# Latent attention scores computed in row halves and row quarters of the systolic array, with a PSUM bank for each head

## The chip, the core and the metric

The kernel runs on one core of a Trainium2 chip. A core has a matrix engine (TensorE, "PE" in the profile, with its weight loads shown as "PEld"), three engines that work on vectors (VectorE "DVE", ScalarE "ACT", GpSimd "POOL") and SyncE ("SP"), which here issues most of the DMA transfers. Each engine runs its own instruction stream in order. TensorE writes its products to PSUM, which has eight banks of 512 fp32 values a partition; DVE and ACT read them from there. The metric is device time in microseconds, the median of several runs.

## The reference, cut to what matters

A decoder block with post-layernorm runs over 32 sequences of 256 tokens with 256 features, in fp32: latent self-attention, cross-attention to 120 context rows, and a mixture of experts with a shared expert. The change concerns the scores of the first part:

```python
Wdkv = x @ latent_w + latent_b                       # [32, 256, 72], keys and values
q = einsum('btc,hcl->bhtl', x, Wd_w) + Wd_b          # 16 heads of 72 features
scores = einsum('bhtl,bsl->bhts', q, Wdkv) / 4       # causal mask, softmax
y = einsum('bhts,bsl->bhtl', attn, Wdkv)
x = layernorm(x + y_as_rows @ out_w + out_b)
x = layernorm(x + cross_attention(x, ctx_1024))      # 16 heads of 64 features
x = layernorm(x + experts(x) + shared(x))
```

Keys and values are the same 72 latent features for every head. Since 72 is more than 64, the kernel stores a head's features as 64 (`LM`) and 8 (`LR`).

## The kernel before, in words

The sequences go through a software pipeline of rounds. Round n computes self-attention of sequence n, the end of it for sequence n-1, and cross-attention of sequences n-1 and n-2. `attention_round` (L795) writes out the order by hand, and within the blocks `manual_schedule` TensorE keeps exactly that order; SyncE keeps it in the start and round 0 only. The other engines' orders come from a scheduler that goes by priority; operations inside `urgent()` go ahead of others.

The sixteen heads are four groups (`g`) of four (`HG`). For a group, `queries` (L345) projects 4 x 64 query features in two blocks of 128 (two heads above each other). ACT (L366) and DVE (L373) move them from PSUM so that each head's 64 features lie in rows 0 to 63 of `qT`. The other 8 features of all 16 heads are projected once a sequence by `query_rest` (L333) into `q8`, and four DMAs a group (L352) copy each head's eight rows into rows 64 to 71 of `qT`. `keys` (L307) gives `kT` with 72 rows.

`scores` (L386) is called three times a group: bank 0 holds the first 128 queries of all four heads against 128 keys; banks 1 and 2 hold the other 128 queries of two heads each against 256 keys. Each matmul contracts 72 rows. DVE adds the mask (L402) and takes the negated maximum (L406); `softmax` (L409) runs an exponential per head on ACT (L412), the reciprocal on DVE (L419), and the scaling on POOL (L420). `turn` (L423) transposes the weights on TensorE, and `weigh` (L449) and `weigh_rest` (L472) multiply them with the values. The first uses two halves of the array's columns, the second four quarters of them. `latent_out` (L489) is the output projection.

For cross-attention, `cross_scores` (L558) already works in pairs: the even head in rows 0 to 63 of the array, the odd in rows 64 to 127, into two banks. `cross_turn`, `cross_weigh` (L596, two halves of the columns) and `cross_out` (L618) follow; `cross_keys` and `cross_values` prepare the context.

PSUM has two pools of banks: `"l"` with two, for `cross_scores`, and `"r"` with six, for everything else (L125). A step waits until a bank of its pool has been read.

After the last round the experts' work (`feed_forward`, L1011) is mixed into the remaining cross-attention by `fill`, and then runs alone.

Of the kernel before, what the change touches and what calls it, by code (L numbers as in the profile page):

```python
# [32 lines left out]
def decoder_kernel(  # L33
# [61 lines left out]
    mask = const.tile([P, 2 * P], F32, name="mask")  # L95
    nc.gpsimd.memset(mask, 0.0)
    nc.gpsimd.affine_select(
        out=mask[:, P:],
        in_=mask[:, P:],
        compare_op=ALU.is_ge,  # L100
        fill=NEG,
        base=0,
        pattern=[[-1, P]],
        channel_multiplier=1,
    )
# [94 lines left out]
    lat_sb = wp.tile([P, DC, L], F32, name="lat_sb")  # L200
    latb = wp.tile([L, 1], F32, name="latb")
# [13 lines left out]

    v_bufs = [wp.tile([P, TC, VW], F32, name=f"v_{k}") for k in range(2)]
# [4 lines left out]
    def first_weights():  # L221


        raw = ow_sb.rearrange("p a b -> p (a b)").rearrange("p (c n) -> p c n", c=DC)
        nc.sync.dma_start(out=lat_sb, in_=latent_w.rearrange("(c p) l -> p c l", p=P))
        nc.sync.dma_start(out=raw, in_=wd_w.rearrange("(c p) n -> p c n", p=P))
        nc.scalar.dma_start(out=latb, in_=latent_b.unsqueeze(1))
        nc.scalar.dma_start(
            out=wdbs[:, ZC - 1 : ZC], in_=wd_b[LM:, :].rearrange("l h -> (l h)").unsqueeze(1)
        )  # L230
        nc.scalar.dma_start(out=wdb_sb, in_=wd_b)
        nc.sync.dma_start(out=outb, in_=out_b.partition_broadcast(P))

    def order_weights():
# [10 lines left out]
        for d in range(DC):  # L245
            nc.vector.tensor_copy(
                wd_sb[:, d, H * LM :].rearrange("p (l h) -> p l h", h=H),
                by_head[:, d, :, LM:].rearrange("p h l -> p l h"),
            )
# [57 lines left out]
    def keys(s):  # L307

        st = states[s]
        pk = bank("r", [L, T], f"pk_{st['nm']}")  # L310
        project(pk, [(lat_sb[:, c, :], st["xT"][:, c, :]) for c in range(DC)])
        st["kT"] = sp.tile([L, T], F32, tag="kT", name=f"kT_{st['nm']}")
        with urgent():
            nc.scalar.activation(st["kT"], pk, AF.Identity, bias=latb)

    def values(s):
# [3 lines left out]
        for t in range(TC):  # L320
            nc.tensor.transpose(
                pv[:, t, :], st["kT"][:, t * P : (t + 1) * P], ident[:L, :L]
# [22 lines left out]
    def queries(s, g):  # L345

        st = states[s]
        qT = sp.tile([L, HG, T], F32, tag="qT", bufs=2, name=f"qT_{st['nm']}_{g}")
        st["qT", g] = qT
        for j in range(HG):  # L350
            h = g * HG + j
            nc.sync.dma_start(  # L352
                out=qT[LM:L, j, :], in_=st["q8"][h::H, :]
            )
# [8 lines left out]
        by_pair = qT[0:LM].rearrange("l (a two) t -> l a two t", two=2)  # L363
        with urgent():
            for a in range(2):
                nc.scalar.activation(  # L366
                    by_pair[:, a, 0, :],
                    pq[0:LM, a, :],
                    AF.Identity,
                    bias=wdbs[0:LM, c0 + a : c0 + a + 1],  # L370
                    scale=QSCALE,
                )
            nc.vector.scalar_tensor_tensor(  # L373
                by_pair[:, :, 1, :],
                pq[LM:P],
                QSCALE,
                wdbs[LM:P, c0 : c0 + 2].unsqueeze(2).to_broadcast([LM, 2, T]),
                ALU.mult,
                ALU.add,
            )  # L380
# [3 lines left out]
    BANKS = ((0, (0, 1, 2, 3)), (1, (0, 1)), (1, (2, 3)))  # L384

    def scores(s, g, k):  # L386
        st = states[s]
        t, js = BANKS[k]
        n, width = len(js), (t + 1) * P
        nm = f"{st['nm']}_{g}_{k}"  # L390
        pS = bank("r", [P, n, width], f"pS_{nm}")
        for a, j in enumerate(js):
            nc.tensor.matmul(  # L393
                pS[:, a, :],
                st["qT", g][:, j, t * P : (t + 1) * P],
                st["kT"][:, 0:width],
                start=True,
                stop=True,
            )
        sm = sp.tile([P, n, width], F32, tag="sm", bufs=5, name=f"sm_{nm}")  # L400
        m = mask[:, 2 * P - width :]
        nc.vector.tensor_tensor(  # L402
            sm, pS, m.unsqueeze(1).to_broadcast([P, n, width]), ALU.add
        )
        nmax = ap.tile([P, n], F32, tag="nmax", bufs=8, name=f"nmax_{nm}")
        nc.vector.tensor_reduce(nmax, sm, AX.X, ALU.max, negate=True)  # L406
        softmax(st, ("sm", g, k), sm, sm, nmax, n, width, nm)
# [15 lines left out]
    def turn(s, g, k):  # L423
# [9 lines left out]
        for j in range(HG):  # L433
            if k == 0:
                block = st["sm", g, 0][:, j, :]
            else:
                block = st["sm", g, 1 + j // 2][:, j % 2, (k - 1) * P : k * P]
# [86 lines left out]
    def cross_values(s, n):  # L524
        st = states[s]
        if n == 0:
            st["vx"] = ap.tile([S2, H, DH], F32, tag="vx", bufs=1, name=f"vx_{st['nm']}")
# [211 lines left out]


# [4 lines left out]
    def first_section(n):  # L745
        run(scores, n, 0, 0)
        run(scores, n, 0, 1)
        run(turn, n - 1, 3, 0)
        run(turn, n - 1, 3, 1)
        run(scores, n, 0, 2)  # L750
        run(turn, n - 1, 3, 2)
        run(queries, n, 1)
        run(cross_turn, n - 2, 4, 1, 0)
        run(cross_turn, n - 2, 4, 1, 1)
# [5 lines left out]
        run(cross_weigh, n - 2, 4)  # L760
        run(latent_out, n - 1)

    def last_section():

        weigh(B - 1, 2)
        for b in range(3):
            turn(B - 1, 3, b)
        weigh(B - 1, 3)
        weigh_rest(B - 1)
        latent_out(B - 1)  # L770
        for odd in range(2):
# [360 lines left out]
```

## Time and profile before

| | |
|---|---|
| median of 3 runs | 3464.92 us (3463.93 to 3467.61) |
| profiled execution, its own time | 3463.73 us |
| its span, first to last instruction | 3461.9 us |
| PE busy | 3435.6 us, 99% |
| weight loads busy | 2615.1 us, 76% |
| DVE, ACT, POOL busy | 1629.3, 1497.2, 1088.7 us |
| granted TensorE clock | 1.000 |
| one middle round | 75.0 us |
| the attention rounds end | at about 2390 us |

A row of a timeline has the start, the length, engine, line, operation, output<-inputs, shapes and how many instructions are merged (x). The shape `72*128 72x256` means 72 rows and 128 columns of the array and a moving operand of 256 columns. Ends of matmuls are modelled and overlap with the next ones, so the difference of two starts says more than the length. A row of a group has the busy time, the mean of one instruction in ns, and the idle time before it with what ended it. A row of the waits reads: engine, what waited, what it waited for, total us, times, longest us.

### The profile page before, as it was taken

To read this page: it belongs to the slowest core of one execution; us is meant where nothing else is said; L and a number is where in the kernel's file an instruction comes from. 1 tells how busy PE (TensorE), PEld (TensorE's weight loads), DVE (VectorE), ACT (ScalarE), POOL (GpSimd) and SP (SyncE) were. 2 spreads that over 40 slices of the span, in tenths; PEclk is the share of its full clock that TensorE was granted. 3 is DMA by queue.
4 is the path that set the end of the run, shared out by engine and by line. 5 is a ranking of instruction groups with operands and counts; after the bars stand their busy time and mean duration, and the time that the engine had idled before them with its cause. 6 is when DMAs were issued, how large, how long until landed. Compare 5 with 4: busy or idle time off the path is not lost.

```text
span 3461.9 us, 58143 instructions
## 1 busy us (share of the span) xinstructions
PE 3435.6 (99%) x21468; PEld 2615.1 (76%) x21468; DVE 1629.3 (47%) x3639; ACT 1497.2 (43%) x5456; POOL 1088.7 (31%) x1073
## 2 busy tenths in 40 slices
PE   8999999999999999999999999999999999999999
PEld 6888888888888888888888888887666656666655
DVE  4555555556555555654555565454311133221133
ACT  4556544555554555554455565445311111111111
POOL 2333322333332233332223333223344411444410
PEclk9999999999999999999999999999999999999999
DMA  3000000000000000000000000002455531455421
GB/s 97 17 16 17 17 17 25 18 20 17 17 17 20 24 17 20 17 17 16 20 24 20 17 17 17 16 17 86 100 123 124 131 97 62 117 123 123 105 82 52
DMA packets 144561, 164.42 MB, mean 47 GB/s; under 512 B 31384, under 2 KB 120216, under 8 KB 144280
## 3 DMA queue, kind: packets, MB, share of 16 engines
q1 hardware_dynamic: 119392, 126.09, 12.2%
q0 software_dynamic: 24576, 34.62, 5.7%
q8 instruction: 171, 2.80, 0.3%
q14 instruction: 110, 0.90, 0.1%
q10 hardware_dynamic: 312, 0.01, 0.0%
HBM read 105.61 MB, written 50.86 MB: 45 GB/s over the span
## 4 chain that ended last, share of the span: by engine, by line
PE 98%; ACT 0%; DMA 0%; DVE 0%; POOL 0%; SPq 0%; issue 0%; POOLq 0%; ACTq 0%
PE po L178 14%; PE pS L393 10%; PE pq L178 7%; PE pqx L178 7%; PE pd L178 6%; PE pg L178 6%; PE pu L178 6%; PE pz L458 5%; PE pT L438 5%; PE pL L565 4%; PE pc L604 3%; PE pxT L588 3%; PE pkx L178 3%; PE pu_s L178 3%; PE pg_s L178 3%; PE pvx L178 3%
## 5 line engine op out<-in xcount | busy, mean ns | idle before, releaser
L420 POOL TENSOR_TENSOR sm<-sm,rs 128x512 f32<-128x512 f32 x384 | 396.6, 1040 | 359.0 <-DVE rs L419 338.2
L412 ACT ACTIVATE sm<-sm,nmax 128x128 f32<-128x128 f32 (+1 forms) x1024 | 461.6, 466 | 18.6 <-DVE nmax L406 17.1
L420 POOL TENSOR_TENSOR xsm_x<-xsm_x,rs_x 128x480 f32<-128x480 f32 x256 | 252.4, 986 | 676.6 <-DVE rs_x L419 672.5
L412 ACT ACTIVATE xsm_x<-pL,nmax_x 128x120 f32<-128x120 f32 x1024 | 359.9, 375 | 124.3 <-DVE nmax_x L575 124.3
L393 PE MATMUL pS<-kT,qT 72*128 72x128 f32 (+1 forms) x2048 | 379.2, 328 | 3.7 <-DMA qT<-q 3.1
L152 POOL TENSOR_TENSOR rstd<-rstd,mhalf 128x2 f32<-128x2 f32 (+1 forms) x97 | 67.1, 692 | 934.1 <-DVE rstd L151 934.1
L393 PEld LDWEIGHTS pS<-kT,qT 72*128 72x128 f32 x2048 | 294.0, 191 | 21.7 <-ACT sm L412 2.8
L944 POOL DMA_INDIRECT acc<-eo,offs x128 | 200.8, 1569 | 342.3 <-DVE eo L941 313.4
L402 DVE TENSOR_TENSOR sm<-pS,mask 128x512 f32<-128x512 f32 x384 | 261.4, 681 | 70.7 <-PE pS L393 64.7
L178 PE MATMUL pq<-xT,wd_sb 128*128 128x256 f32 x1152 | 276.9, 381 | 0.0
L534 ACT COPY vx<-pvx 120x512 f32<-120x512 f32 x64 | 37.5, 585 | 549.5 <-PE pvx L178 549.5
L406 DVE TENSOR_REDUCE nmax<-sm 128x2 f32<-128x512 f32 (+1 forms) x384 | 258.6, 674 | 2.4
L178 PE MATMUL po<-ow_sb,zT 128*128 128x256 f32 x1152 | 257.2, 382 | 0.0
L1008 DVE TENSOR_TENSOR hT<-gl,pu 128x512 f32<-128x512 f32 x128 | 88.0, 688 | 341.6 <-PE pu L178 197.2
L178 PEld LDWEIGHTS po<-ow_sb,zT 128*128 128x128 f32 x1152 | 216.2, 190 | 40.1 <-DVE cxT L616 8.8
L178 PE MATMUL pg<-xeT,wg 128*128 128x512 f32 x512 | 240.8, 593 | 0.0
L178 PE MATMUL pu<-xeT,wu 128*128 128x512 f32 x512 | 240.6, 592 | 0.0
L178 PE MATMUL pqx<-x1T,wq_sb 128*128 128x256 f32 x1024 | 234.8, 382 | 0.0
L178 PEld LDWEIGHTS pq<-xT,wd_sb 128*128 128x128 f32 x1152 | 209.5, 191 | 25.0 <-issue 0.2
L178 PE MATMUL pd<-wd,hT 128*128 128x256 f32 x1024 | 226.6, 379 | 0.0
L178 PE MATMUL po<-wo_sb,cxT 128*128 128x256 f32 x1024 | 226.3, 379 | 0.0
L412 ACT ACTIVATION_READ_ACCUMULATOR xsm_x<-pL,nmax_x 128x1 f32 x1024 | 225.6, 220 | 0.0
(130 smaller groups left out, 5790.5 us busy)
## 6 DMA issues: line engine op xcount, KB each, us to landing
wg<-in_wg_dram SPq DMA_DIRECT2D x32, 512.0 KB
wu<-in_wu_dram SPq DMA_DIRECT2D x32, 512.0 KB
wd<-in_wd_dram SPq DMA_DIRECT2D x32, 512.0 KB
x<-in_x_dram SPq DMA_DIRECT2D x32, 256.0 KB
qT<-q SPq DMA_DIRECT2D x512, 8.0 KB
rows<-x SPq DMA_DIRECT2D x32, 256.0 KB
acc<-x SPq DMA_DIRECT2D x32, 256.0 KB
x2t<-x2T SPq DMA_DIRECT2D x32, 256.0 KB
```

The source lines that it names most:

```text
L178: nc.tensor.matmul(acc, lhsT, rhs, start=(i == 0), stop=(i == n - 1))
L393: nc.tensor.matmul(pS[:, a, :], st["qT", g][:, j, t * P : (t + 1) * P], st["kT"][:, 0:width], start=True, stop=True,)
L402: nc.vector.tensor_tensor(sm, pS, m.unsqueeze(1).to_broadcast([P, n, width]), ALU.add)
L406: nc.vector.tensor_reduce(nmax, sm, AX.X, ALU.max, negate=True)
L412: nc.scalar.activation(dst[:, a, :], src[:, a, :], AF.Exp, bias=nmax[:, a : a + 1], accum_out=rs[:, a, :],)
L420: nc.gpsimd.tensor_tensor(dst, dst, rs.to_broadcast([P, n, width]), ALU.mult)
L438: nc.tensor.transpose(pT[:, j, :], block, ident)
L458: nc.tensor.matmul(pz[odd * LM : (odd + 1) * LM, a, k * P :], st["v"][:, k, 0:LM], moving(st, g, 2 * a + odd, k), start=(k == 0), stop=(k ...
L565: nc.tensor.matmul(pLs[odd][:, j, :], st["qxT", c0][rows, j, t * P : (t + 1) * P], st["kxT"][rows, c0 + j, :], start=True, stop=True,)
L588: nc.tensor.transpose(pT[:, j, :], st["xsm", c0, t, odd][:, j, :], ident)
L604: nc.tensor.matmul(pc[odd * DH : (odd + 1) * DH, a, :], st["vx"][:, 2 * (c0 + j0 + a) + odd, :], st["xpt", c0, odd][:, j0 + a, :], start=True,
L944: nc.gpsimd.indirect_dma_start(out=acc[b], out_offset=self.rows(b), in_=eo[:, k, :], in_offset=None, compute_op=ALU.add,)
```

## The change

The scores of a head are now two sums into one bank. The eight extra features of four heads are contracted in the four row quarters of the array at once: head j of a group uses rows 32j to 32j+31. For that the columns of the extra query weights, and so the rows of `q8`, are put in the order (j, l, g), and a new tile `kr` holds the eight key rows in the same places, with zeros in the rows of the other groups. `keys` projects them four times (`LW` = 96 columns), and `place_keys` spreads them with four DMAs. The 64 main features are contracted in the two row halves: the even head in rows 0 to 63, the odd in rows 64 to 127. The queries can then stay as they were projected, and a copy of the keys, `kD`, is kept in the lower half. The DMAs from `q8` to `qT` fall away.

`scores` is called once a group and takes four `"r"` banks, one for each head, 128 + 256 columns. The mask has three blocks. The maximum, the reciprocal and the scaling run over all four heads, once for 128 columns and once for 256. The round is laid out anew: `cross_scores` follows each `scores`, a `cross_weigh` or `weigh` precedes three of the four, and `cross_out` is in the second quarter of the round. The start of the kernel has a written order on all engines.

```diff
+    LW = LM + HG * LR
+    lat_sb = wp.tile([P, DC, LW], F32, name="lat_sb")
...
+    kr = wp.tile([P, NG, T], F32, name="kr")
+    nc.gpsimd.memset(kr, 0.0)
...
+        nc.scalar.dma_start(out=latb[0:L], in_=latent_b.unsqueeze(1))
+        for j in range(1, HG):
+            nc.scalar.dma_start(
+                out=latb[LM + j * LR : LM + (j + 1) * LR], in_=latent_b[LM:].unsqueeze(1)
+            )
+        by_column = wd_b[LM:, :].rearrange("l (g j o) -> j (l g) o", j=HG, o=1)
+        for j in range(HG):
+            nc.sync.dma_start(
+                out=wdbs[j * 32 : (j + 1) * 32, ZC - 1 : ZC], in_=by_column[j]
+            )
+        nc.vector.tensor_copy(
+            lat_sb[:, :, L:].rearrange("p c (j l) -> p c j l", l=LR),
+            lat_sb[:, :, LM:L].unsqueeze(2).to_broadcast([P, DC, HG - 1, LR]),
+        )
...
     def keys(s):
-        pk = bank("r", [L, T], f"pk_{st['nm']}")
+        pk = bank("r", [LW, T], f"pk_{st['nm']}")
+        st["kD"] = sp.tile([P, T], F32, tag="kD", name=f"kD_{st['nm']}")
         with urgent():
             nc.scalar.activation(st["kT"], pk, AF.Identity, bias=latb)
+            nc.vector.tensor_scalar(st["kD"][LM:], pk[0:LM], latb[0:LM], None, ALU.add)
+    def place_keys(s):
+        for g in range(NG):
+            nc.sync.dma_start(out=kr[g::NG, g, :], in_=states[s]["kT"][LM:, :])
...
     def queries(s, g):
-        for j in range(HG):
-            h = g * HG + j
-            nc.sync.dma_start(
-                out=qT[LM:L, j, :], in_=st["q8"][h::H, :]
-            )
...
-            nc.vector.scalar_tensor_tensor(
-                by_pair[:, :, 1, :],
...
+    SEG = (slice(0, P), slice(P, 3 * P))
+    def scores(s, g):
+        pS = [bank("r", [P, 3 * P], f"pS_{nm}_{j}") for j in range(HG)]
+        for t in range(TC):
+            for j in range(HG):
+                rows = slice(j * 32, (j + 1) * 32)
+                nc.tensor.matmul(
+                    pS[j][:, SEG[t]],
+                    st["q8"][rows, t * P : (t + 1) * P],
+                    kr[rows, g, 0 : (t + 1) * P],
+                    start=(t == 0),
+                    stop=False,
+                )
+        for a in range(2):
+            for t in range(TC):
+                for odd in range(2):
+                    rows = slice(odd * LM, (odd + 1) * LM)
+                    k = st["kD"] if odd else st["kT"]
+                    nc.tensor.matmul(
+                        pS[2 * a + odd][:, SEG[t]],
+                        st["qT", g][rows, a, t * P : (t + 1) * P],
+                        k[rows, 0 : (t + 1) * P],
+                        start=False,
+                        stop=(t == TC - 1),
+                    )
+        sm = sp.tile([P, HG, 3 * P], F32, tag="sm", bufs=2, name=f"sm_{nm}")
+        for j in range(HG):
+            nc.vector.tensor_tensor(sm[:, j, :], pS[j], mask, ALU.add)
+        for t in range(TC):
+            nc.vector.tensor_reduce(nmax[:, t, :], sm[:, :, SEG[t]], AX.X, ALU.max, negate=True)
+            for j in range(HG):
+                nc.scalar.activation(
+                    sm[:, j, SEG[t]], sm[:, j, SEG[t]], AF.Exp,
+                    bias=nmax[:, t, j : j + 1], accum_out=rs[:, t, j, :],
+                )
+            nc.vector.reciprocal(rs[:, t], rs[:, t])
+            block = sm[:, :, SEG[t]]
+            nc.gpsimd.tensor_tensor(
+                block, block, rs[:, t].to_broadcast([P, HG, (t + 1) * P]), ALU.mult
+            )
...
-            st["vx"] = ap.tile([S2, H, DH], F32, tag="vx", bufs=1, name=f"vx_{st['nm']}")
+            st["vx"] = ap.tile([S2, H, DH], F32, tag="vx", bufs=2, name=f"vx_{st['nm']}")
...
+    def attention_round(n):
+        run(cross_weigh, n - 2, 0)
+        scores(n, 0)
+        run(cross_scores, n - 2, 4, 1)
+        (turn n-1,3 x3; cross_turn n-2,4,0 x2; weigh n-1,2; weigh n-1,3; weigh_rest n-1)
+        if routed(n):
+            route((n - 3) // BQ)
+        run(latent_out, n - 1)
+        (load and load_context n+1; cross_turn n-2,4,1 x2; cross_values n-1 x2)
+        (cross_keys n,0; turn_x1 n-1; queries n,1; score; cross_queries n-1 x4)
+        run(cross_weigh, n - 2, 4)
+        scores(n, 1)
+        run(cross_scores, n - 1, 0, 0)
+        (turn n,0 x3; queries n,2; cross_out n-2)
+        scores(n, 2)
+        run(cross_scores, n - 1, 0, 1)
+        (turn n,1 x3; cross_turn n-1,0,0 x2; queries n,3; turn_x2 n-2)
+        (turn_x, keys, query_rest n+1; weigh n,0; weigh n,1)
+        scores(n, 3)
+        run(cross_scores, n - 1, 4, 0)
+        (turn n,2 x3; place_keys, values n+1; queries n+1,0)
+        (cross_turn n-1,0,1 x2; cross_keys n,1)
...
+    every = {getattr(mybir.EngineType, n) for n in ("PE", "SP", "DVE", "Activation", "Pool")}
+    with tc.manual_schedule(engines=every):
         load(0)
...
-        unit.hT = fp.tile([P, FC, cols], F32, tag="hT", name=f"hT_{unit.nm}")
+        unit.hT = fp.tile([P, FC, cols], F32, tag="hT", bufs=1, name=f"hT_{unit.nm}")
```

In the diff, lines in brackets of `attention_round` name the calls in short. The last section and the mixing of the first experts with the end of cross-attention are reordered to match.

## The prediction

> **What bounds the kernel now.** I read the page's first and fourth parts first, then TensorE's waits.
>
> ```profile
> span 3461.9 us, 58143 instructions
> PE 3435.6 (99%) x21468; PEld 2615.1 (76%) x21468; DVE 1629.3 (47%) x3639; ACT 1497.2 (43%) x5456; POOL 1088.7 (31%) x1073
> PE 98%; ACT 0%; DMA 0%; DVE 0%; POOL 0%; SPq 0%; issue 0%; POOLq 0%; ACTq 0%
> ...
> PE pk L178 <- DVE xT L172: 6.9, 1, 6.9
> PE pxT L168 <- DMA x<-in_x_dram: 4.0, 1, 4.0
> PE pS L393 <- DMA qT<-q: 3.1, 2, 2.4
> ```
>
> TensorE is the bound and waits for almost nothing: the chain is 98% PE, its waits sum to some 18 us, nearly all in the first 30. So what counts is the time from one matmul's start to the next. The page's means (379 ns for pS) are modelled latencies and overlap, so I take differences of starts. Here is TensorE's timeline around one group of four heads; each fp32 matmul leaves two records, called passes here, each with its weight load.
>
> ```profile
> 1514.89 1.92 PE L393 MATMUL pS<-kT,qT 72*128 72x128 f32 x12
> 1516.65 1.04 PE L438 MATMUL pT<-ident,sm 128*128 128x128 f32 x8
> 1517.53 1.03 PE L393 MATMUL pS<-kT,qT 72*128 72x256 f32 x4
> 1518.39 0.60 PE L438 MATMUL pT<-ident,sm 128*128 128x128 f32 x4
> ```
>
> The scores take 1516.65-1514.89 plus 1518.39-1517.53 = 2.62 us. In the records' starts a pass of 128 columns takes 0.112 us and one of 256 takes 0.216: 8 x 0.112 + 8 x 0.216 = 2.62. The eight transposes between (one record each) take 0.88, 0.109 each. Two existing steps show what packing does: the cross scores (two halves of 64 rows) and weigh_rest (four columns' quarters).
>
> ```profile
> 1511.24 0.81 PE L178 MATMUL pqx<-x1T,wq_sb 128*128 128x256 f32 x3
> 1511.98 1.16 PE L565 MATMUL pL<-kxT,qxT 64*128 64x120 f32 x16
> 1513.06 0.48 PE L178 MATMUL pqx<-x1T,wq_sb 128*128 128x256 f32 x1
> ...
> 1558.43 2.81 PE L479 MATMUL pzr<-pt,v 128*32 128x256 f32 x64
> 1561.17 0.44 PE L604 MATMUL pc<-xpt,vx 120*64 120x256 f32 x2
> ```
>
> The 16 pL records are 8 pairs, both halves starting 7 ns apart and the next pair 0.111 later: 0.89 us, and 1513.06-1511.98 = 1.08 shows 0.19 more. That is the price of changing the array's division. The 64 pzr records are 16 quads: 8 x 0.216 + 8 x 0.109 = 2.60 of the 2.74 shown. A quad costs what one pass costs.
>
> **The stream of the scores.** scores (L386) loses 8 passes of each width. It gains 4 heads x 2 blocks of 8 features in quarters, so with quads at one pass's price 2 x 0.112 + 2 x 0.216 = 0.656 us; and 64 features in halves, four pairs of two passes: 4 x 0.112 + 4 x 0.216 = 1.312. Together 1.968 against 2.624: -0.656 a group, x 128 groups = **-84.0 us**. Pairs of 64 rows are seen in pL, at 120 columns. Four row quarters into four banks at once are not seen here; the nearest row is pzr, four column quarters. The bounds are 0.656 (quads) and 1.312 (only pairs run together: +84.0 in all, no saving).
>
> **A rule against it.** The Trainium skill, "TensorE: Matmul & The Clock Gate", section Measured speedup vs the span model, gives four row tiles of 32 rows a measured 3.07 times, not 4. By it the quarters take 2.624/3.07 = 0.855 us, +0.199 a group, +25.5 us in all, and the forecast would be 3442. I take the row: pzr's quads lose nothing in an unbroken stream. The rule stays as a case.
>
> **Changes of division.** From the starts of all records, as the drain ahead plus the weight load laid bare: full to 64 columns 0.145, 64 to 32 columns 0.124, 32 to 64 columns 0.164, columns to full 0.20, full to row halves 0.189, 64 columns to row halves 0.196, row halves to the turns 0.155, to a projection 0.202. A round now has 13: weigh, weigh_rest, cross_weigh, latent_out (0.637), four visits of cross_scores (0.391, 0.344, 0.344 and, with weigh ahead and keys behind, 0.543): 2.26 us. After the change there are 18. Scores enter quarters (0.196, once 0.189), then halves (0.196), cross_scores follows in halves for nothing, and the turns leave (0.155): 0.547, 0.547, 0.540, 0.547. Columns are entered for weigh 2 (0.145), weigh_rest (0.124), left for latent_out (0.20), and entered for cross_weigh twice and weigh 0 (3 x 0.145): 3.09 us. +0.826 a round, x 32 = **+26.4 us**. Quarters are put at what halves cost, as the exposed load has the same 128 columns; 0.1 either way is 13 us.
>
> **The softmax behind the scores.** All four heads now go through in one block each of 128 and 256 columns. DVE: four adds of 384 (between 0.41 at 256 and 0.69 at 512, 0.47 net of overlap), reduces of 0.6 and 1.2. POOL: 1.04 and, by 733 ns at 256 and 1040 at 512, 1.65. ACT's exponentials are the same. All lie beside PE; what matters is that they are in time. The stretches between scores in the middle round, one row each, the last one long:
>
> ```profile
> 1514.90:1524.90 10.00, 10.00 (x82) 9.09 (x81) 8.21 (x18) 8.26 (x38) 5.09 (x5) 1.00 0.02 5
> 1524.90:1539.30 14.40, 14.40 (x122) 11.82 (x121) 10.14 (x20) 10.54 (x42) 6.39 (x7) 1.00 0.06 20
> 1539.30:1549.00 9.70, 9.70 (x79) 8.78 (x78) 7.70 (x18) 9.22 (x40) 5.09 (x5) 1.00 0.03 8
> 1549.00:1589.90 40.90, 40.90 (x287) 32.73 (x287) 15.27 (x36) 13.25 (x48) 6.44 (x8) 1.00 0.08 24
> ```
>
> The columns are length, PE, PEld, DVE, ACT and POOL busy, clock and DMA. ACT is at 9.22 of 9.70 in the third, so a tight place exists. Moving cross_out (6.9 us) into the first stretch makes the distances from the end of scores to the next cross_scores 13.3, 12.7 and 11.1 us, by the same prices. The third is: cross pairs 0.89, turns 1.46, values 0.14, queries 1.73, cross_turn 0.87, cross_keys 1.78, cross_weigh 1.87, scores 2.36. Before that next cross_scores both "l" banks must have been read by ACT. ACT starts about 2.0 us after scores end (last two adds, first reduce), then needs, by distances of starts, 4 x 0.39 + 4 x 0.51 for exponentials, 8 x 0.35 for the cross ones, one late turn copy 0.47, queries 0.73, cross turn 0.46, kxT 0.44: 8.5. That ends at 10.5 against 11.1. The turns need 2.0 + 1.56 + 2.04 + 1.7 of copies + 0.2 + 1.65 = 9.2 of 12.4. So the cover is 0.6 us, and an order of ACT that runs late by more goes straight to PE. Queued behind a waiting cross_scores are turn, cross_turn and weigh; next late would be latent_out. I take 0.2 us for 30 rounds, **+6 us**, between 0 and 1.5 a round (0 to 45).
>
> A second rule, "TensorEngine Tiling (Array Packing)", section PSUM Bottleneck, says that evacuation may become the bottleneck after packing. DVE reads pS for 4 x 0.47 = 1.9 us a group, against 3 x 0.6 = 1.8 now, in stretches of at least 11 us of which it is busy about 8; by the row it adds nothing, by the rule the 2 us before the softmax could grow, which the 0 to 1.5 holds.
>
> **Four banks at once.** Six "r" banks rotate. Ahead of the four scores come two cross_weigh or weigh tiles (or a query and cross_out), 1.7 us or more of PE after the next older ones (pqx, pq8, pkx, turns). Their copies take 0.6 to 0.7. Cost 0; if a copy queues behind exponentials, up to 0.5 a round, in the range above.
>
> **Keys.** keys projects 96 columns for 72, same passes; kD is one DVE operation of some 0.41 and takes the place of four of 0.69 (L373). place_keys issues 4 DMAs of 32 KB a round on SP, where queries issued 16 of 8 KB. kr has one buffer: the fourth waits for the last quarters of scores(n, 3), and loads and stores queued later on SP wait with it. Due at scores(n+1, 0), 10 us on. In the first round the rows from q (ready 15.92) let pS start at 17.91: some 2 us a small transfer, 2 to 4 here, hidden. Were it late, PE would wait at once. One hT buffer costs nothing: the next write follows pu, which PE runs after the last down. A second vx only frees.
>
> **Start and first rounds.** The waits for qT in round 0 go (3.1 DMA, 0.4 DVE and some unattributed: -4). But round 0 has no cross work between scores: turn(0, 0) comes 5.7 us after scores(0, 0) end, its second block is ready after 7.5; the same at turn(0, 1): about +3.5. In round 1 cross_scores(0, 0, 1) comes 6.2 us after its forerunner, whose banks are read after some 10: +4. First weights: four small SP DMAs, three on ACT, one DVE copy; DVE now in written order, so xT's copy no longer waits behind the weights (the 6.9 above), but query_rest still needs them at about 10 us. 0. Sum **+3.5**, between -4 and +10. The tail has the same work in another order: 0, 3 us either way.
>
> **Sum.** -84.0 + 26.4 + 6 + 3.5 = -48.1 against the profiled execution's 3463.7 (span 3461.9 and 1.8 around it): 3415.6. The median is 1.2 above it: **3417**.
>
> **Rivals.** (1) Quads by the rule: 3442. For it: no row of four row tiles here; against it: pzr. (2) ACT and the "l" banks late by 1 us a round: +24 on my sum, 3441; for it: ACT's 95% in one stretch and the 0.6 us of cover; against it: the longer first stretch, and PE's waits for ACT today are nearly none. The two overlap in time. (3) Slower: the quarters do not stream, the four tiles' writes to four banks go two by two. Place: the eight passes ahead of each group. Price: 3417 + 84 = 3501. It decides from 48/84 of the way, a quad at 1.57 passes. For it: no evidence that four banks are written at once; against it: pairs into two banks lose nothing. A milder form of (2), 1.8 us a round, ends at the old time. (4) No change: gain and late softmax cancel, 3465.
>
> **How the numbers follow.** My forecast with its own range (3400 to 3436, stalls 0 to 0.8 a round) 0.58; (1) or (2) 0.19; within 0.2% 0.07; slower 0.16, by (3) 0.09 or (2) worse than 1.8. 0.2% (7 us) is about what a measurement of this kernel can tell. Faster 0.77, same 0.07, slower 0.16. The range starts at 3398: no stall and first rounds at -4 give 3403, and 0.03 less a change of division 5 less again. It reaches to 3490, short of most of (3), so that about 2 in 10 is left out.
>
> **What would show it.** Records of pS in 32-row form, four starts within some 20 ns and the next quad 0.112 or 0.216 later: the stream; 0.15 or more, the rule. First-pass starts at the entry: 0.2. Waits of PE pL on ACT xsm_x, or of pT on POOL sm, over 6 us in all: rival 2. Waits of pS on DMA kr: place_keys late. A sum over PE of starts that is right with a total that is not would put the error in the start or tail.

## The result and the profile after

The changed kernel takes 3585.61 us (median of 4 runs, 3583.82 to 3585.84) against 3466.18 for the kernel before on the same chips: ratio 1.0344, 95% interval 1.0326 to 1.0362. It is 119 us slower where 48 us faster was forecast. The profiled execution took 3585.64 us. From the page of the changed kernel, its span, TensorE's busy time and the chain that ended last:

```profile
span 3583.9 us, 60589 instructions
...
PE 3471.2 (97%) x23516; PEld 2572.2 (72%) x23516; DVE 1538.5 (43%) x3416; ACT 1481.1 (41%) x5456; POOL 1064.9 (30%) x947
...
PE 75%; DVE 14%; ACT 8%; issue 1%; POOL 1%; DMA 0%; SPq 0%; POOLq 0%; ACTq 0%; DVEq 0%
```

The chain was 98% PE; now almost a quarter of it runs through DVE and ACT. PE's busy share fell only from 99% to 97%: the modelled ends of matmuls cover a part of each wait. TensorE's waits in the changed kernel, with their total, their number and the longest:

```profile
PE pk L180 <- DVE xT L174: 56.1, 32, 1.9
PE pz L497 <- DVE pt L481: 5.7, 25, 0.2
PE pT L477 <- POOL sm L446: 5.6, 3, 2.2
PE pxT L170 <- DVE pt L481: 5.5, 29, 0.2
PE px2T L170 <- ACT pt L483: 5.1, 30, 0.2
PE pL L604 <- ACT xsm_x L454: 4.8, 5, 1.4
```

What happened once before (6.9 us, in the start) happens in every round: `keys` waits for the copy of `xT`, which `turn_x` has only just handed to DVE. The lines of `pxT` and `px2T` are the same lateness, seen from PSUM banks that ACT and DVE have not read yet. The middle round, cut at the starts of its four `scores` (columns: length, PE, PEld, DVE, ACT and POOL busy, granted clock, DMA):

```profile
1502.40:1515.70 13.30, 13.30 (x102) 11.49 (x100) 6.15 (x13) 8.61 (x37) 4.18 (x4) 1.00 0.01 1
1515.70:1533.00 17.30, 15.09 (x129) 11.33 (x128) 10.83 (x25) 9.80 (x40) 7.58 (x8) 0.90 0.16 53
1533.00:1544.80 11.80, 11.80 (x116) 9.64 (x114) 8.52 (x23) 7.24 (x29) 2.21 (x2) 1.00 0.02 4
1544.80:1581.40 36.60, 36.60 (x293) 29.01 (x292) 13.94 (x32) 15.10 (x57) 8.24 (x8) 1.00 0.04 11
```

The forecast had 13.3, 12.7 and 11.1 us for the first three. The first is exact, the second is 4.6 us too long, and in it alone the granted clock is below 1. Here is that stretch in the timeline of the changed kernel:

```profile
1515.74 0.94 PE L410 MATMUL pS<-kr,q 32*128 32x128 f32 x16
1515.85 0.69 DVE L667 TENSOR_TENSOR r<-po,x 128x512 f32<-128x512 f32 x1 [0.65 <-PE po L180]
...
1516.61 0.37 PE L422 MATMUL pS<-kT,qT 64*128 64x128 f32 x1
...
1518.03 1.05 PE L604 MATMUL pL<-kxT,qxT 64*128 64x120 f32 x16
1518.56 0.73 DVE L156 TENSOR_SCALAR x<-r,mv,rstd 128x256 f32<-128x256 f32 x2 [0.81 <-POOL rstd L154]
...
1519.21 1.94 DVE L431 TENSOR_TENSOR sm<-pS,mask 128x384 f32<-128x384 f32 x4
...
1521.96 0.40 ACT L437 ACTIVATE sm<-sm,smax 128x128 f32<-128x128 f32 x1 [6.97 <-DVE smax L435]
...
1525.90 0.68 DVE L174 COPY xT<-pxT 128x512 f32<-128x512 f32 x1
...
1526.72 0.64 PE L180 MATMUL pk<-xT,lat_sb 128*96 128x256 f32 x2 [1.85 <-DVE xT L174]
```

The layernorm of `cross_out` (L667 to L156) now stands directly ahead of `scores(n, 2)`, so DVE is still busy with it, and for 0.81 us waiting for POOL's step of it, when the scores are done. The four adds of the mask begin at 1519.21, 1.2 us after PE has gone on to the cross scores. ACT, idle for 6.97 us, gets its first exponential 3.9 us after the scores end (1518.03 to 1521.96); in the stretch before this one it is 2.3. Everything that the two engines do behind it (copies of the turns, `x2T`, `xT`) is late by that, and `turn_x` has nothing between itself and `keys` any more. Here they start 2.5 us apart, 1.85 of it the wait. In the profile of before they start 6.1 us apart, with two `weigh`, a `cross_weigh` and a `cross_scores` between them:

```profile
1531.43 0.60 PE L168 MATMUL pxT<-ident,x 128*128 128x128 f32 x4
1531.96 2.82 PE L458 MATMUL pz<-pt,v 128*64 128x256 f32 x32
1534.61 1.90 PE L604 MATMUL pc<-xpt,vx 120*64 120x256 f32 x16
1536.44 1.16 PE L565 MATMUL pL<-kxT,qxT 64*128 64x120 f32 x16
1537.53 1.08 PE L178 MATMUL pk<-xT,lat_sb 128*72 128x256 f32 x4
```

The clock, by the same columns, in three neighbouring windows of that stretch:

```profile
1524.00:1527.40 3.40, 1.35 (x8) 0.99 (x8) 2.58 (x6) 3.40 (x13) 2.39 (x3) 1.00 0.05 17
1527.40:1530.80 3.40, 3.40 (x14) 2.07 (x14) 0.83 (x3) 3.40 (x19) 2.78 (x3) 0.51 0.21 68
1530.80:1534.20 3.40, 3.40 (x50) 2.44 (x48) 0.87 (x2) 0.97 (x4) 1.06 (x2) 0.99 0.11 29
```

PE was busy for 1.35 of 3.40 us, and in the next 3.4 us its clock is half. `pk`, `pq` and the first `pz` in it take 1.7 us longer than the same passes elsewhere. So the stalls of 2.9 us in this stretch cost 4.6, which is what it is too long by.

**Where the time went.** For every pass I subtract from the distance to the next start what such a pass takes in an unbroken stream (0.109 to 0.112 us at 128 columns, 0.216 at 256, 0.429 at 512). The excess goes to a half-speed window (3.4 us in which the granted clock is 0.5) if it lies in one, else to a change of division if the neighbour has another one, else to waits.

| us | changes of division | waits | half-speed windows | span |
|---|---|---|---|---|
| before | 75.0 | 20.7 | 0 | 3461.9 |
| after | 116.8 | 149.0 | 36.1 | 3583.9 |
| e3_both | 126.2 | 80.7 | 10.2 | 3499.1 |
| e5_old_scores | 92.5 | 107.8 | 15.9 | 3582.4 |
| e10_cover_weigh | 117.0 | 60.8 | 5.5 | 3465.6 |
| e13_both_on_vector | 116.8 | 33.1 | 5.1 | 3437.0 |

After less before: 41.8 + 128.3 + 36.1 - 84.0 (the stream, as forecast) = +122.2; the spans differ by 122.0. The saving was made, and 206 us were lost elsewhere. A wait that ends beside a change of division is booked as a change, so the line between these two columns is rough.

### The profile page after: what moved, and what is told of

It reads as the page before. It is cut to its first block, busy times and chain, and to the rows that moved or that the text cites. A ratio compares the mean times of both kernels' runs of the same rounds, so it can differ in the third digit from the quotient of the medians.

```text
span 3583.9 us, 60589 instructions
## 1 busy us (share of the span) xinstructions
PE 3471.2 (97%) x23516; PEld 2572.2 (72%) x23516; DVE 1538.5 (43%) x3416; ACT 1481.1 (41%) x5456; POOL 1064.9 (30%) x947
## 4 chain that ended last, share of the span: by engine, by line
PE 75%; DVE 14%; ACT 8%; issue 1%; POOL 1%; DMA 0%; SPq 0%; POOLq 0%; ACTq 0%; DVEq 0%
PE po L180 13%; PE pqx L180 6%; PE pd L180 6%; PE pu L180 6%; PE pg L180 6%; DVE sm L431 5%; PE pq L180 5%; PE pz L497 4%; DVE smax L435 3%; ACT sm L437 3%; PE pu_s L180 3%; PE pg_s L180 3%; PE pfo L180 3%; PE pvx L180 3%; PE pzr L518 2%; ACT xsm_x L454 2%
## 5 line engine op out<-in xcount | busy, mean ns | idle before, releaser
L446 POOL TENSOR_TENSOR sm<-sm,srs 128x512 f32<-128x512 f32 (+1 forms) x256 | 375.4, 1466 | 1448.4 <-DVE srs L444 1255.2
L437 ACT ACTIVATE sm<-sm,smax 128x128 f32<-128x128 f32 (+1 forms) x1024 | 459.2, 451 | 586.7 <-DVE smax L435 586.7
L180 PE MATMUL pq<-xT,wd_sb 128*128 128x256 f32 x1152 | 294.5, 399 | 1.8 <-DVE wd_sb L266 1.8
L431 DVE TENSOR_TENSOR sm<-pS,mask 128x384 f32<-128x384 f32 x512 | 249.5, 547 | 90.5 <-PE pS L422 90.2
L180 PEld LDWEIGHTS pq<-xT,wd_sb 128*128 128x128 f32 x1152 | 221.5, 201 | 32.4 <-DVE wd_sb L266 2.6
L435 DVE TENSOR_REDUCE smax<-sm 128x4 f32<-128x512 f32 (+1 forms) x256 | 232.2, 947 | 4.4
L180 PE MATMUL pqx<-x1T,wq_sb 128*128 128x256 f32 x1024 | 227.0, 380 | 0.0
L180 PEld LDWEIGHTS po<-wo_sb,cxT 128*128 128x128 f32 x1024 | 194.5, 190 | 26.9 <-issue 0.5
L180 PEld LDWEIGHTS pqx<-x1T,wq_sb 128*128 128x128 f32 x1024 | 194.4, 191 | 26.9 <-issue 0.8
L180 PEld LDWEIGHTS pd<-wd,hT 128*128 128x128 f32 x1024 | 192.1, 190 | 27.5 <-DVE hT L1034 1.8
```

What stands on the lines that cost most here:

```text
L180: nc.tensor.matmul(acc, lhsT, rhs, start=(i == 0), stop=(i == n - 1))
L431: nc.vector.tensor_tensor(sm[:, j, :], pS[j], mask, ALU.add)
L435: nc.vector.tensor_reduce(nmax[:, t, :], sm[:, :, SEG[t]], AX.X, ALU.max, negate=True)
L437: nc.scalar.activation(sm[:, j, SEG[t]], sm[:, j, SEG[t]], AF.Exp, bias=nmax[:, t, j : j + 1], accum_out=rs[:, t, j, :],)
L446: nc.gpsimd.tensor_tensor(block, block, rs[:, t].to_broadcast([P, HG, (t + 1) * P]), ALU.mult)
```

## The experiments

Each ratio is against the kernel before on the same chip. The line numbers are those of the changed kernel unless an edit shifts them.

### Two orders in the second stretch

**e1_turnx_early** moves `turn_x` away from `keys`, ahead of `cross_out`; **e2_norm_early** moves `cross_out` into the stretch's beginning, so that its layernorm is over before `scores(n, 2)`; **e3_both** does both.

```diff
         run(cross_scores, n - 1, 0, 0)
+        run(cross_out, n - 2)             # e2, e3
         for b in range(3):
             turn(n, 0, b)
         queries(n, 2)
+        run(turn_x, n + 1)                # e1, e3
-        run(cross_out, n - 2)             # e2, e3
...
         run(turn_x2, n - 2)
-        run(turn_x, n + 1)                # e1, e3
         run(keys, n + 1)
```

> The changed kernel with turn_x(n+1) moved ahead of cross_out(n-2), so that keys(n+1) no longer follows it at once. Theory 1 (adjacency: keys right behind turn_x makes TensorE wait 1.9 us a round for the copy of xT, and that wait brings the windows at half clock): the wait of pk on xT goes (61 us), the windows at half clock of the rounds go (some 32 us), 3585 falls to about 3490. Theory 2 (DVE late: the layernorm behind cross_out holds DVE while the adds of scores(n, 2) wait, and everything after is late): the wait moves on to the next steps of the same stretch (turn_x2, query_rest, weigh), and the time stays above 3545.

> The changed kernel with cross_out(n-2) moved ahead of turn(n, 0) and queries(n, 2), 3.4 us earlier, so that its layernorm is over when scores(n, 2) end; turn_x and keys stay together. Theory 2 (DVE late): the adds of scores(n, 2) start about 2.4 us earlier against the scores, the wait of pk on xT falls to 0.6 us or less and the waits of px2T and weigh go: about 3480. Theory 1 (adjacency): the wait of pk stays at 0.9 us or more, as the copy takes 0.7 after the transposes, and only the half clock goes: about 3520.

> Both moves. If the two causes are all there is, the stream of the prediction is left: 3417 to 3440, under the time of before. If the softmax in one block for four heads is late in itself, waits of turn, cross_scores or weigh remain and it stays above 3460.

e1: 3527.97 us, ratio 1.0180 (1.0163 to 1.0197). e2: 3512.29, 1.0136 (1.0119 to 1.0153). e3: 3498.45, 1.0091 (1.0074 to 1.0107). Both causes are real: 58 and 73 us. They overlap, since together they give 87. The two largest steady waits of PE in e1:

```profile
PE pc L643 <- ACT xpt L631: 10.8, 30, 0.4
PE pz L497 <- DVE pt L481: 5.8, 25, 0.2
```

In e1 the wait of `pk` for `xT` is gone, and the excess in half-speed windows falls from 36.1 to 5.2 us. But another wait, of `cross_weigh` for a copy on ACT, has grown and now leads the list: that step takes 2.91 us a round, in the changed kernel 2.51, elsewhere 1.88. In e2 `pk` still waits for `xT` (33.7 us, 32 times, at most 1.1) and the half-speed windows cost 8.5: the stall is as frequent and shorter. The softmax of that stretch is in time again: the adds begin while the scores still run, and ACT starts 2.3 us after they end (1476.57).

```profile
1476.11 1.95 DVE L431 TENSOR_TENSOR sm<-pS,mask 128x384 f32<-128x384 f32 x4 [0.24 <-PE pS L422]
1476.57 1.05 PE L604 MATMUL pL<-kxT,qxT 64*128 64x120 f32 x16
1478.87 0.40 ACT L437 ACTIVATE sm<-sm,smax 128x128 f32<-128x128 f32 x1 [3.64 <-DVE smax L435]
```

e3 has neither, and still takes 76.1 us a round where the kernel before takes 75.3 (rounds 3 to 30). So I had found the first two causes, not all.

### Which half of the change brings the waits

**e4_old_round** puts the new `scores` into the order of the old round and tail; **e5_old_scores** puts the old scores (with the old keys, queries and softmax, six `sm` buffers instead of five) into the new round and tail.

```diff
 # e4, in the old round
-        run(scores, n, 0, 0)
-        run(scores, n, 0, 1)
-        run(turn, n - 1, 3, 0)
-        run(turn, n - 1, 3, 1)
-        run(scores, n, 0, 2)
-        run(turn, n - 1, 3, 2)
+        run(scores, n, 0)
+        for b in range(3):
+            run(turn, n - 1, 3, b)
 # e5, in the new round
-        scores(n, 0)
+        for k in range(3):
+            scores(n, 0, k)
```

> The new scores alone, in the round and the tail of the kernel before (scores in one call where it was three, turns after it; place_keys after the turns of the fourth quarter). Changes of division: four scores that enter quarters, then halves, and leave to the turns add 4 x 0.54 us a round, 69 us, against 84 of stream: 3450 if no wait is added. If four banks at once or the softmax in one block make TensorE wait by themselves, 3480 or more.

> The other half: the scores of the kernel before (72 rows, three banks, with their DMAs and softmax) in the new round and tail, with six buffers for sm. If the new round itself carries the waits (turn_x with keys behind it, the layernorm of cross_out ahead of scores(n, 2)), pk waits about 2 us a round here too, windows at half clock appear, and with about 20 us more of changes of division the time is 3550 or more. If the waits come from the softmax in one block for four heads, pk hardly waits and the time is 3480 to 3500.

e4: 3544.90, 1.0227 (1.0210 to 1.0244). e5: 3587.25, 1.0346 (1.0328 to 1.0363). PE's first wait in e5:

```profile
PE pk L178 <- DVE xT L172: 78.4, 32, 7.6
```

The new round alone, without the new scores, costs as much as the whole change, by the same wait. In e4 it is not there; two others are:

```profile
PE pT L477 <- DVE sm L431: 20.3, 32, 2.5
...
PE pS L410 <- ACT xpt L631: 6.5, 27, 0.3
```

Both are waits for banks: `turn` directly behind the scores takes one that the mask's adds have still to read, and `scores` takes one that holds a cross turn (single `pS` steps last 3.0 us where 2.28 is usual). These named waits are 27 us. The same account of e4 puts some 70 us more than before on the changes of division, close to the 69 expected, and some 90 on waits and half-speed windows, against 84 saved. So the new scores do not pay in the old order either, and the new round, as it was laid out, loses more than they save. Which waits a round has is a property of its order, and neither half can be judged alone.

### Following the waits

In e3 the largest wait is the one of `cross_weigh(n-2, 0)` for the odd heads' copy from `cross_turn(n-1, 0, 1)`. **e6_odd_first** takes the odd head first, to see whether it is the pairing that costs; **e7_turn_early** moves `cross_turn` ahead of `turn(n, 2)`.

```diff
 # e6, cross_weigh
-                for odd in range(2):
+                for odd in (1, 0):
 # e7
         run(cross_scores, n - 1, 4, 0)
+        for odd in range(2):
+            run(cross_turn, n - 1, 0, 1, odd)
         for b in range(3):
             turn(n, 2, b)
         run(place_keys, n + 1)
         run(values, n + 1)
         run(queries, n + 1, 0)
-        for odd in range(2):
-            run(cross_turn, n - 1, 0, 1, odd)
         cross_keys(n, 1)
```

> As with both moves (3498), but cross_weigh issues the odd head ahead of the even one, so that the first matmul of each pair waits for the operand that comes later (the odd heads' xpt from ACT). If a pair whose second half waits stays out of step to the end of the step, the passes that run alone go and the cross_weigh ahead of scores(n, 0) falls by 0.43 us, 13 us in all: 3485. If only the wait itself costs, nothing changes: 3498.

> As with both moves, with cross_turn(n-1, 0, 1) moved ahead of turn(n, 2), so that its copy on ACT is long done at cross_weigh(n-1, 0). If this wait is the largest that is left, cross_weigh falls from 2.9 us to 1.9, about 30 us: 3468. If ACT is only late as a whole, the wait moves to the turns and to the banks of cross_scores and under 10 us are gained.

e6: 3499.35, 1.0093 (1.0076 to 1.0110): nothing. The passes that ran without their partner are gone, and the wait by name has grown from 10.4 to 29.2 us. The step costs what the copy is late, either way. e7: 3499.13, 1.0091 (1.0075 to 1.0108): `cross_weigh` is back at 1.88 us, and this wait has come up instead:

```profile
PE pq L180 <- DVE xpt L633: 26.2, 30, 0.9
```

`queries(n+1, 0)` now takes the bank of `cross_turn`, which DVE has not read yet. The wait has only changed its name.

**e8_spread** (from e7), **e9_cover** (from e7) and **e10_cover_weigh** (from e9) spread steps that wait for nothing over the stretches, and put work that is already due between a step and its consumer. All three also take a new order for the end of the attention: `cross_weigh(last-1, 4)` and `cross_out(last-1)` go ahead of `turn_x1(last)`, which waited 3.7 us for a layernorm.

```diff
 # e8: cross_keys(n, 0) to the end of the round
-        run(cross_values, n - 1, 0)
-        run(cross_values, n - 1, 1)
-        cross_keys(n, 0)
-        run(turn_x1, n - 1)
+        run(cross_weigh, n - 2, 4)
         queries(n, 1)
+        run(turn_x1, n - 1)
...
         run(turn_x, n + 1)
+        run(cross_values, n - 1, 0)
...
         run(turn_x2, n - 2)
+        run(cross_values, n - 1, 1)
         run(keys, n + 1)
 # e9: as e8, but cross_keys(n, 0) stays, cross_turn(n-1, 0, 1) is behind turn(n, 2), and
+        cross_keys(n, 0)
+        run(cross_weigh, n - 2, 4)
+        run(turn_x1, n - 1)
+        queries(n, 1)
 # e10: the values stand ahead of weigh(n-1, 2) and behind turn_x
             run(cross_turn, n - 2, 4, 0, odd)
+        run(cross_values, n - 1, 0)
         run(weigh, n - 1, 2)
...
         run(turn_x, n + 1)
-        run(cross_values, n - 1, 0)
+        run(cross_values, n - 1, 1)
...
         run(turn_x2, n - 2)
-        run(cross_values, n - 1, 1)
```

> As the one before, with work spread over the four stretches: cross_values go from the long stretch to the first and second, cross_keys(n, 0) to the third, cross_weigh(n-2, 4) ahead of queries(n, 1), and in the tail cross_out stands between latent_out and turn_x1. More TensorE work lies behind each softmax. If waits are all that separates the change from its stream, 3415 to 3440, faster than before by about 1%. If the changes of division cost more than counted, or ACT stays late, 3450 or more.

> As the spread round (3512), whose trace has three waits left in every round: cross_queries right behind turn_x1 (0.95 us), cross_weigh(n-2, 4) right behind cross_turn (0.98), queries behind cross_turn in the fourth stretch for a bank (0.65). Each step gets work between it and the copy it needs: cross_keys(n, 0) ahead of cross_weigh, queries(n, 1) behind turn_x1, the turns ahead of cross_turn. If these covers are all that is missing, 2.4 us a round go and the time is about 3437, faster than before by 0.8%. If waits only move on, as they did in the runs before, 3480 or more.

> As the one before, with cross_values(n-1, 0) between cross_turn and weigh(n-1, 2), so that the copies behind the turns are done, and cross_values(n-1, 1) in the second stretch, none in the third. The wait of 0.2 to 0.5 us at weigh goes; the third stretch is 1.7 us shorter, so cross_scores after it may wait 0.3 us for its banks. If ACT has room, 3430; if the third stretch was already at its limit, 3445.

e8: 3511.63, 1.0128 (1.0111 to 1.0145). It repaired the tail (1080.1 us from the last `latent_out` to the end; 1085.2 after the change, 1080.0 before) and made the rounds worse: `cross_queries` behind `turn_x1` (23.7 us in 32 waits for `x1T`) had lost the `queries` that covered it. e9 gives that cover back: 3470.53, 1.0012 (1.0005 to 1.0019), 41 us less than e8 but 33 above what was expected. e10: 3466.39, 1.0000 (0.9991 to 1.0009), also above the 3430 to 3445 expected, with one large wait left, `pq` for the first turn's bank (15.6 us in 30).

**e11_keys_ahead** (from e10) puts `cross_keys(n, 1)` between `turn(n, 2)` and `cross_turn(n-1, 0, 1)`, so that the queries get another bank. **e12_copy_on_vector** (from e11) gives one copy to DVE, **e13_both_on_vector** (from e12) a second.

```diff
 # e11
             turn(n, 2, b)
+        cross_keys(n, 1)
         for odd in range(2):
             run(cross_turn, n - 1, 0, 1, odd)
         run(place_keys, n + 1)
         run(values, n + 1)
         run(queries, n + 1, 0)
-        cross_keys(n, 1)
 # e12, cross_turn
-            if odd:
+            if odd and (c0, t) != (0, 1):
                 nc.scalar.copy(dst, pT)
             else:
                 nc.vector.tensor_copy(dst, pT)
 # e13, queries
             for a in range(2):
+                if g == 0:
+                    nc.vector.tensor_scalar(
+                        q[:, a, :], pq[:, a, :], QSCALE, wdbs[:, c0 + a : c0 + a + 1], ALU.mult, ALU.add
+                    )
+                    continue
                 nc.scalar.activation(
```

> Edit against e10_cover_weigh: the second half of the cross keys (n, 1) is moved from the round's end to the place between turn(n, 2) and cross_turn(n-1, 0, 1), so that the projection behind values is no longer the one that takes the bank of the first turn, whose copy ACT makes late; queries(n+1, 0) takes a younger bank. In e10_cover_weigh that wait is the largest one left: 15.6 us by name, 0.66 a round by the starts of PE, some 20 us. Theory (each wait left can be taken away by putting hidden work ahead of it): it goes, about 3446, ratio 0.994. Rival (the sum of the waits belongs to the chain scores, softmax, turn, weigh, which is longer than what can be put beside it, so that it only changes its name): 3460 to 3470, and some other step of the round's last quarter waits about as long.

> Edit against e11_keys_ahead: the copy of the odd heads of cross_turn(n-1, 0, 1) goes to DVE; it was on ACT, queued behind four exponentials of the same softmax. In e11_keys_ahead TensorE's wait of 0.66 us a round had only moved from queries(n+1, 0) to cross_weigh(n-2, 0) (2.56 us where 1.88 is usual: the second matmul of its first pair waits for that copy, and the rest of the step stays out of step) and 0.36 more to the scores behind it. DVE has nothing to do at that moment but two small copies. Theory (the wait is one of a queue on ACT): cross_weigh is back at 1.88, scores at 2.28, cross_scores at 0.98 to 1.33; by starts 0.7 to 1.0 us a round less, about 3437 to 3448, ratio 0.992 to 0.995. Rival (only the name changes again): 3460 to 3470.

> Edit against e12_copy_on_vector: the two copies of queries(n+1, 0) from PSUM, with their bias, go to DVE; they were on ACT, behind the exponentials. In e12_copy_on_vector the scores(n+1, 0) wait for them: 10.6 us by name, and 3.16 us for that scores where the other three take 2.28, so 0.88 a round, 28 us in all. Theory (ACT's queue in the round's last quarter is late by about 1 us, and DVE's is not): scores is back at 2.28, the round from 75.1 to about 74.2, 3462 - 28 = 3434, ratio about 0.991. Rival (only the name changes again): 3455 to 3466.

e11: 3468.48, 1.0005 (0.9996 to 1.0013). The wait has moved again, to `cross_weigh`. Its cause, in e11's timeline:

```profile
1546.79 0.54 ACT L561 COPY kxT<-pkx 128x480 f32<-128x480 f32 x1
...
1547.23 0.51 ACT L437 ACTIVATE sm<-sm,smax 128x256 f32<-128x256 f32 x1
...
1547.67 2.63 PE L643 MATMUL pc<-xpt,vx 120*64 120x256 f32 x16
1547.73 0.57 ACT L631 COPY xpt<-pxT 120x512 f32<-120x512 f32 x1
```

The copy that `pc` needs stands on ACT behind the copy of the cross keys and an exponential, while DVE is nearly free. The waits of e3 (`pc` for `xpt`), e10 (`pq` for `pt`) and e11 have this in common: in the round's last quarter it is a copy in ACT's queue that is late, by something under 1 us, whichever bank or tile shows it. (The waits of e7 and e8 for `xpt` were for copies on DVE, and this does not cover them.) e12: 3461.75, 0.9988 (0.9980 to 0.9996). `cross_weigh` is back at 1.88 us, but the next wait comes up, as the rival had it:

```profile
PE pS L410 <- ACT qT L388: 10.6, 27, 0.5
```

`pS` does not read `qT` in its first passes; it waits for the bank that ACT is to clear by writing `qT`. e13 gives that to DVE too: **3438.77 us, 0.9920 (0.9906 to 0.9934)**. Nothing comes in its place in an ordinary round. The page of e13:

```profile
span 3437.0 us, 60541 instructions
...
PE 3399.3 (99%) x23516; PEld 2542.6 (74%) x23516; DVE 1593.2 (46%) x3512; ACT 1448.2 (42%) x5362; POOL 1068.2 (31%) x947
...
PE 92%; ACT 4%; DVE 3%; DMA 0%; issue 0%; POOL 0%; SPq 0%; POOLq 0%; ACTq 0%; DVEq 0%
```

And its middle round, in the same cuts as above:

```profile
1491.90:1507.40 15.50, 15.50 (x109) 12.59 (x108) 9.81 (x22) 8.34 (x36) 6.86 (x7) 1.00 0.00 1
1507.40:1519.70 12.30, 12.30 (x125) 10.18 (x124) 8.23 (x16) 8.28 (x32) 2.75 (x3) 1.00 0.24 76
1519.70:1530.80 11.10, 11.10 (x112) 9.29 (x110) 8.91 (x20) 8.24 (x38) 4.20 (x5) 1.00 0.05 14
1530.80:1565.30 34.50, 34.50 (x290) 27.87 (x288) 13.25 (x30) 14.79 (x56) 8.51 (x8) 1.00 0.03 9
```

73.4 us, at full clock, against 79.0 and 75.0. This version beats both kernels: 0.8% under the kernel before, 4% under the changed one.

What is left of waits in e13's rounds lies mostly in three of them (rounds 10, 18 and 26), which take 78.2, 77.1 and 78.7 us where the ordinary ones take 73.5. There `turn` waits:

```profile
PE pT L482 <- DVE sm L436: 6.2, 3, 2.1
PE pT L482 <- POOL sm L451: 4.4, 3, 1.9
...
786.40 1.05 PE L609 MATMUL pL<-kxT,qxT 64*128 64x120 f32 x16
789.60 0.41 DVE L758 MATCH_REPLACE8 left<-best,left 128x256 f32<-128x256 f32 x1
789.93 0.55 DVE L436 TENSOR_TENSOR sm<-pS,mask 128x384 f32<-128x384 f32 x1
790.53 0.66 PE L482 MATMUL pT<-ident,sm 128*128 128x128 f32 x4 [2.06 <-DVE sm L436]
```

The timeline is that of the first of the three. The scores end at 786.40, but the selection of the experts' tokens (L755 to L758) is at work on DVE, and the first add of the mask starts 3.5 us later. It is the same lateness as the layernorm's, with other work on DVE ahead of the adds. No run moved that work.

## Why the prediction was wrong, by its own steps

**What bounds the kernel**: right, and with it the use of differences of starts; they account for the whole result.

**The stream of the scores** (-84.0): right. In the timeline above the quarters start at 1515.74 and the halves at 1516.61: 0.87 us, the 0.656 of the sum and 0.21 for one change of division. The halves take 1.42, the 1.312 and 0.11 more at their first pair, where a weight load is laid bare. Four row quarters into four banks cost what one pass costs; the rule of 3.07 times, and with it rivals 1 and 3, do not show.

**Changes of division** (+26.4): the prices were right, the total was not. A round of the changed kernel, where nothing is late, pays 3.2 us for them (3.09 forecast), the round before 2.25 (2.26). The measured total grew by 41.8, not 26.4. By the prices some 29 of that are the changes themselves; the rest comes where a pass beside a change had to wait, which this account books there. In e13 the round pays 3.4, as `cross_weigh(n-2, 4)` no longer stands directly ahead of scores.

**The softmax behind the scores** (+6, 0 to 45): this is the step that failed. It named three distances and worked out only the third, on the grounds that ACT is fullest there. For the second it took over 12.7 us as a length of PE's work, without laying out DVE's queue for it. It said that ACT starts about 2.0 us after the scores end; there it is 3.9, because the layernorm of `cross_out`, which the same step moves, stands in DVE's queue ahead of the adds. The step counted `cross_out` as 6.9 us of PE put into a stretch and not as the DVE and POOL instructions it issues. e2 shows the size: 73 us for this order alone, of which 28 are half-speed windows. The third stretch, the one worked out, took 11.8 for 11.1: 0.7 lost where 0.2 was put and 1.5 allowed, nearly all of it in `cross_weigh`'s wait for ACT. Together, waits and half-speed windows grew by 164 us where the steps for late softmax and start had 9.5.

**A cover that no step named**: `turn_x` lost the 6.1 us between itself and `keys`. The prediction treated the keys' columns, DVE's copy and the four DMAs, and not the step that feeds them. That is the wait of 56.1 us, 1.75 by 32, in the list; e1 shows 58 us for it, half-speed windows included. e5, with the old scores in the new round, has this wait too: the order makes it, not the new scores.

**The clock**: no step allowed for it, since the profile of before has 1.000 in all its rounds. The stalls were followed by half-speed windows that cost 36.1 us more, some 6 of them in the start and the tail.

**Four banks** (0): right in the changed kernel. Its bound of 0.5 us a round was too small: in e12 a copy queued behind exponentials cost 0.88. **Keys**: the DMAs to `kr` are in time as forecast; none is in the waits. **Start and first rounds** (+3.5): the first `latent_out` starts at 67.4 us for 63.6, +3.8. That is in part luck: 3.1 of it are two half-speed windows, at 29 and 39 us, which the step did not have, and in the traces of the other runs with the new scores that point lies anywhere from 61.1 to 67.3. The step's own terms were not measured singly. **Tail** (0, 3 either way): +5.2, outside; 3.7 of it is `turn_x1(last)` waiting behind a layernorm, with only `cross_turn` and two `cross_values` between it and `latent_out`.

**The rivals**: 2 and its milder form had the right kind, a late softmax, but in the wrong place (ACT and the `"l"` banks, 4.8 us in all in 5 waits) and with a limit of 1.8 us a round; the rounds lost 3.6 on the kernel before, 5.2 on the forecast. Its sign, those waits and the ones of `pT` for POOL over 6 us in all, did come (4.8 + 5.6), but from a few rounds and not as a cost of each. The slower case rested mostly on quarters that don't stream; its smaller part, rival 2 worse than 1.8 us, came nearest, with the place still wrong.

**The forecast as a possibility**: e13 has the new scores and a round near the forecast's, 73.4 us for the sum's 75.0 - 2.62 + 0.83 + 0.19 = 73.4 in the middle, and reaches 3438.8, not 3417. Over rounds 3 to 30 it averages 74.35; the account puts what is left into the changes of division (41.8 for 26.4) and 12.4 us more of waits than before and 5.1 in half-speed windows, against 9.5 forecast for late softmax and start. The three rounds with the selection hold some 13 us of this. I have not shown that the last 20 us can be had.

## What to carry to other kernels

When a step is moved in a written order, lay out what it issues on every engine, and check each stretch, not just the fullest: a short chain on VectorE and POOL ahead of a softmax makes the softmax late, here by 1.6 us a round. For each moved pair of producer and consumer, write down what lay between them before and what lies there after. When a wait keeps coming back under other names, look for a queue that the names have in common; here moving two copies to a nearly idle engine ended what e7 and e11 had only moved about.

## What the runs showed of the hardware

**Half speed after a part-idle window.** In the changed kernel's profile the half-speed stretches last 3.413 us each and lie on one fixed grid of that step. Of the grid windows from 60 us on to the last 10 us, those in which PE stood idle (by starts) for 2.18 us or more, 17 of them, were all followed by a half-speed window. Of those with between 1.75 and 2.14 us, one was, at 2.06. One more half-speed window directly follows another. Counted in the same way, the other traces agree: every full-speed window with over 2.1 us idle was followed by one at half speed, and none with under 1.8. The Trainium skill, "TensorE: Matmul & The Clock Gate", section What's actually happening, has a free-running window of 3413 ns and a half-rate clock after an idle one, which agrees with the grid. Its section HAM oscillation asks only that gaps be under some 3.4 us. Here the longest wait of `pk` is 1.9 us, and with the smaller gaps around it it is enough: by the measurement a window need not be idle as a whole, about 2.2 us of 3.4 suffices. By that section's rule the stalls of the rounds would have cost some 30 us less.

**A wait inside a group of tiles shows less than it costs.** In e11 `cross_weigh` waits 0.49 us by the profile (on its weight loads) and takes 0.68 longer (2.56 for 1.88); in e12 `scores` waits 0.40 and takes 0.88 longer. While one tile of a pair or a quad waits, its partners run on alone, and that time is lost to the packing. e6 shows that the loss is the lateness itself and not the order of the pair. A list of waits therefore understates those of packed matmuls; differences of starts don't.
